# Starting the second group's front end inside the first group's serial chain, and reordering the first transfers

## The chip, the cores and the metric

The kernel runs on one core of one Trainium2 chip. The metric is the device time of one execution in microseconds (us); lower is better. TensorE is written PE below, VectorE DVE, ScalarE ACT, GpSimd POOL, and SyncE, which issues most of the DMAs, SP.

## The reference, cut to what matters

The input is 16 sequences of 256 tokens with 128 channels, 4096 tokens in all, in float32. A Mamba layer is followed by a small dense FFN, and then by eight experts that every token goes through:

```python
xz = layernorm(x) @ in_proj_w.T;  xi, z = split(xz)             # 256 + 256 channels
xc = silu(causal_conv4(xi) + conv_b)                            # per channel, 4 taps
dt, B, C = split(xc @ x_proj_w.T, [8, 24])                      # 8 + 16 + 16 columns
dt = softplus(dt @ dt_proj_w.T + dt_proj_b)
h_t = exp(dt_t * A) * h_(t-1) + dt_t * B_t * xc_t               # 16 states per channel
y_t = sum_n h_t[n] * C_t[n]
x1 = x + ((y + D * xc) * silu(z)) @ out_proj_w.T
x2 = layernorm(x + x1 + relu(layernorm(x1) @ w1.T + b1) @ w2.T + b2)
out = layernorm(x2 + sum over 8 experts of (silu(x2 @ Wg[e]) * (x2 @ Wu[e])) @ Wd[e])
```

## The kernel before, in words

The tokens are cut into eight **groups** g of 512 tokens (two sequences). Channels or states lie on the 128 partitions and tokens on the free axis, so nearly every tile is 128x512 floats. For each group there are four pieces of work, written as Python generators that issue some instructions and `yield`:

- `stage_a(g)`: layer norm (statistics on DVE at L167 to L171, a power on POOL at L173, `nb` on DVE at L179, the normalised `xh` on ACT at L185), four transposes on PE into `pxn`, `xn` on ACT (L244). Then two `stage_conv` generators, one for each half of the 256 inner channels: a projection `pi` on PE (L316), the first tap `hc` on ACT (L319), three more taps on DVE (L326), a tanh on ACT (L334), and `xc` on DVE (L336). Then `pd` on PE (L262), its copy `dbc` on ACT (L267), a store of the 32 rows of B and C to a DRAM tile `bc`, issued by ACT (L270), two `pv` matmuls (L276), `dt` on ACT (L278), its softplus on ACT with a table load (L282), `u` on POOL (L286), and the gate `zg` from `pz` (L298, L304, L307).
- the **scan**: 32 states k for each group, 16 for each half. `fetch` (L347) loads B and C from `bc`, broadcast to all partitions, for two states at a time, 512 KB each, into three buffers. `front` makes `dA` on ACT (L354) and `dBx` on POOL (L356, four buffers). `back` runs the recurrence on DVE (L362) and multiplies with C (L364, `hC`). `sum_states` transposes each `hC` into the sum `y` on PE (L369).
- `stage_c(g)`: gate, output projection `po`, norm, FFN (`pf`, `pff`), norm, and the transposed result `x2T` (L478).
- the **experts**: 32 slices j for each group; each makes `pg` and `pu` on PE (L488, L490), tanh and copy on ACT, two products on DVE and POOL, and adds to `acc` on PE (L518).

The order on each engine is written out by hand: the schedule is manual and engines run their instructions in program order. A prologue runs `stage_a(0)` alone until its `dt` and `u` are there (`while "ready" not in ...`, L549). Then comes one main loop (L567); each pass issues one scan state, and one expert slice when a group's `x2T` exists, and advances the generators in `running` by fixed half steps. `limit[0]` caps how many PSUM banks the generators may hold, through `take`. Group g+1 is prepared while group g is scanned; `stage_a(1)` starts in pass k = 1 of group 0, `stage_a(g+1)` in pass 11 of group g for the others. Expert slices of group 0 run beside the scan of group 1, and so on.

All loads of inputs stand at the head of SP's queue: x of groups 0 and 1, the small weights, and then the eight experts with three transfers of 256 KB each (L143 to L146). The first `fetch` calls (L555) come after those 24 in SP's order:

```python
for k in range(0, FETCH, NC):
    fetch(0, k)
```

Of the kernel before, what the change touches and what calls it, by code (L numbers as in the profile page):

```python
# [9 lines left out]
AF = mybir.ActivationFunctionType  # L10
# [8 lines left out]
KC = 4  # L19
# [3 lines left out]
NE = 8  # L23
NF = 4
NC = 2
# [5 lines left out]
FETCH = 4  # L31
START_A = 11
NB = 4
EPS = 1e-5
FAR = 1e28
SLOW = 1e-25
# [3 lines left out]
def kernel(  # L40
# [99 lines left out]
    wg = const.tile([P, NE, NF * P], FP, tag="wg", name="wg")  # L140
    wu = const.tile([P, NE, NF * P], FP, tag="wu", name="wu")
    wd = const.tile([P, NE, NF, DM], FP, tag="wd", name="wd")
    for e in range(NE):  # L143
        nc.sync.dma_start(out=wg[:, e, :], in_=Wg[e])
        nc.sync.dma_start(out=wu[:, e, :], in_=Wu[e])
        nc.sync.dma_start(out=wd[:, e], in_=Wd[e].rearrange("(f p) d -> p f d", p=P))  # L146

    def prepare():

# [57 lines left out]
    def done(name):  # L207
        held.remove(name)
        give(name)
# [15 lines left out]
    def stage_a(g):  # L225
        xt = x_tiles[g]
        s = state[g] = {}
        yield
        stats = norm_stats(xt, f"a{g}")
        yield  # L230
        yield
        scale = norm_shift(stats, f"a{g}")
        yield
        xh = wide("xh", f"xh{g}", 2)
        norm_apply(xt, as4(xh), scale)
        yield
        if g > 0:
            yield
            yield
        pt = yield from take(f"pxn{g}")  # L240
        transpose(pt, as4(xh))
        yield
        xn = wide("xn", f"xn{g}", 2)
        nc.scalar.activation(xn, pt, AF.Identity, bias=b1_sb[:, 0:1], scale=g1_sb[:, 0:1])  # L244
        done(f"pxn{g}")
        yield
        s["xc"] = act.tile([P, NH, TB], FP, tag="xc", name=f"xc{g}")
        for h in range(NH):
            conv = stage_conv(g, h, xn)
            next(conv)  # L250
            next(conv)
            running.append([conv, False])
        while (NH - 1) not in s.get("conv", ()) or 0 not in s["conv"]:
            yield
            yield
        if g > 0:
            yield
            yield
        R = DTR + 2 * NS
        pd = yield from take(f"pd{g}")  # L260
        for h in range(NH):
            nc.tensor.matmul(  # L262
                pd[0:R, :], lhsT=xpw[:, h, :], rhs=s["xc"][:, h, :], start=(h == 0), stop=(h == NH - 1)
            )
        yield
        dbc = act.tile([R, TB], FP, tag="dbc", bufs=1, name=f"dbc{g}")
        nc.scalar.copy(dbc, pd[0:R, :])  # L267
        done(f"pd{g}")
        bc = s["bc"] = dram.tile([2 * NS, TB], FP, tag="bc", name=f"bc{g}")
        nc.scalar.dma_start(out=bc, in_=dbc[DTR:R, :])  # L270
        yield
        dt = s["dt"] = act.tile([P, NH, TB], FP, tag="dt", name=f"dt{g}")
        u = s["u"] = act.tile([P, NH, TB], FP, tag="u", name=f"u{g}")
        for h in range(NH):
            pv = yield from take(f"pv{g}_{h}")
            nc.tensor.matmul(pv, lhsT=dtw[:, bass.ts(h, P)], rhs=dbc[0:DTR, :], start=True, stop=True)  # L276
            yield
            nc.scalar.activation(dt[:, h, :], pv, AF.Identity, bias=dtb[:, h : h + 1])  # L278
            done(f"pv{g}_{h}")
            if h == 0:  # L280
                yield
        nc.scalar.activation(dt, dt, AF.Softplus)  # L282
        yield
        zg = s["zg"] = act.tile([P, NH, TB], FP, tag="zg", name=f"zg{g}")
        for h in range(NH):
            nc.gpsimd.tensor_tensor(u[:, h, :], dt[:, h, :], s["xc"][:, h, :], ALU.mult)  # L286
            if h == NH - 1:

                nc.gpsimd.memset(dt.rearrange("p h (b l) -> p (h b) l", l=L)[:, :, 0:1], FAR)
                s["ready"] = True  # L290
            elif g > 0:
                yield
                yield
        for h in range(NH):

            pz = yield from take(f"pz{g}_{h}")
            for c in range(NTT):
                nc.tensor.matmul(  # L298
                    pz[:, bass.ts(c, P)], lhsT=xn[:, bass.ts(c, P)], rhs=inw[:, bass.ts(NH + h, P)],
                    start=True, stop=True,  # L300
                )
            yield
            tz = wide("tz", f"tz{g}_{h}", 1)
            nc.scalar.activation(tz, pz, AF.Tanh, scale=0.5)  # L304
            yield

            nc.vector.scalar_tensor_tensor(zg[:, h, :], tz, 1.0, pz, ALU.add, ALU.mult)  # L307
            done(f"pz{g}_{h}")
        yield

    def stage_conv(g, h, xn):

        s = state[g]
        yield
        pi = yield from take(f"pi{g}_{h}")
        nc.tensor.matmul(pi, lhsT=inw[:, bass.ts(h, P)], rhs=xn, start=True, stop=True)  # L316
        yield
        hc = wide("hc", f"hc{g}_{h}", 2)
        nc.scalar.activation(  # L319
            hc, pi, AF.Identity, bias=cb[:, h : h + 1], scale=cw[:, h, KC - 1 : KC]  # L320
        )
        yield
        hv = hc.rearrange("p (b l) -> p b l", b=NSEQ)
        pv = pi.rearrange("p (b l) -> p b l", b=NSEQ)
        for k in range(1, KC):
            nc.vector.scalar_tensor_tensor(  # L326
                hv[:, :, k:], pv[:, :, : L - k], cw[:, h, KC - 1 - k : KC - k], hv[:, :, k:],
                ALU.mult, ALU.add,
            )
            if g > 0 and k == KC - 2:  # L330
                yield
                yield
        yield
        nc.scalar.activation(pi, hc, AF.Tanh)  # L334
        yield
        nc.vector.scalar_tensor_tensor(s["xc"][:, h, :], pi, 1.0, hc, ALU.add, ALU.mult)  # L336
        done(f"pi{g}_{h}")
        s.setdefault("conv", set()).add(h)
        yield
# [209 lines left out]
    while "ready" not in state.get(0, {}):  # L549
        if rounds == 1:  # L550
            running.append([prepare(), False])
        half()
        half()
        rounds += 1
    for k in range(0, FETCH, NC):  # L555
        fetch(0, k)
    skip(0, 0)
    for k in range(AHEAD):
        front(0, k)
# [7 lines left out]
    while added < NG * NJ or running:  # L567
        in_scan = t < len(scans)
        in_experts = j < len(slices)
        limit[0] = 1 if in_experts else 2  # L570
        if in_scan:
            g, k = scans[t]
            if k == 0 and 0 < g and g + 1 < NG:
                load_x(g + 1)
            if k == (START_A if g > 0 else 1) and g + 1 < NG:
                running.append([stage_a(g + 1), False])
            t2 = t + FETCH
            if t2 < len(scans) and t2 % NC == 0:
                if "bc" not in state.get(scans[t2][0], {}):
                    raise ValueError("B and C are fetched before they are made")  # L580
                fetch(*scans[t2])
        half()
        if in_experts:
            up(*slices[j])
        half(quick=True)
        half(quick=True)
        lag = LAG_Y if in_experts else 1
        while summed <= min(t - lag, len(scans) - 1):
            gs, ks = scans[summed]
            if ks % NS == 0 and summed:  # L590
                gb, kb = scans[summed - 1]
                gate(gb, kb // NS)
                launch(stage_y(gb, 0) if kb // NS == 0 else stage_c(gb), kb // NS == 1)
            sum_states(gs, ks)
            summed += 1
            if summed == len(scans):
                gate(gs, 1)
                launch(stage_c(gs), True)
        if j > multiplied:
            hidden(*slices[multiplied])  # L600
            multiplied += 1
        if in_scan:
            back(g, k)
            t2 = t + AHEAD
            if t2 < len(scans):
                front(*scans[t2])
                if t2 + 1 < len(scans) and scans[t2 + 1][1] % NS == 0:
                    skip(scans[t2 + 1][0], scans[t2 + 1][1] // NS)
        if in_experts:
            half_gate(*slices[j])  # L610
            j += 1
        if added < (multiplied - 1 if in_experts else multiplied):
            gd, jd = slices[added]
            down(gd, jd)
            added += 1
            if jd == NJ - 1:
                launch(stage_e(gd))
        half()
        if not in_experts:
            half(quick=True)  # L620
            half(quick=True)
        if queued < NG and "x2T" in state.get(queued, {}):
            slices += [(queued, n) for n in range(NJ)]
            queued += 1
        t += 1
# [44 lines left out]
```

## Time and profile before

| | |
|---|---|
| median of three runs | 1095.85 us (1095.71 to 1100.99) |
| the profiled execution | 1096.13 us, its span 1094.3 us |
| busy share of the span | PE 90%, DVE 72%, POOL 65%, ACT 59% |
| mean granted PE clock | 0.952 |
| DMA | 147.03 MB, mean 134 GB/s |
| first instruction of the recurrence (L362) | 35.76 us after the span's start |
| last `hC` of group 0 (L364) | starts at 109.67 us |
| `x2T` of group 0 (L478) | starts at 144.06 us |

A timeline row has the start, the duration, the engine, the source line, the operation, what it writes and reads, the shapes and a count; in brackets stands how long the engine was idle before it and what released it. "SPq" and "ACTq" are DMA issues: they show when a transfer was issued, not when it landed. A windows row has a stretch of the span, its length, the busy time (and instructions) of PE, PEld, DVE, ACT and POOL in this order, the granted PE clock, the DMA engines' busy share, and GB/s. In the page the strips of digits are tenths for 40 equal slices of the span, 27.4 us each.

### The profile page before, as it was taken

How to read it: one execution, taken by the hardware profiler on the slowest of the kernel's cores; microseconds unless marked ns; L12 is line 12 of the kernel's file. 1: busy time of each engine (PE TensorE's matmuls, PEld its weight loads, DVE VectorE, ACT ScalarE, POOL GpSimd, SP SyncE). 2: the span in 40 equal slices, each digit the busy share in tenths (PEclk: the TensorE clock that was granted, in tenths of full speed). 3: DMA queues.
4: the chain of work that ended last, by engine and by line, in shares of the span. 5: the costliest groups of instructions: out<-in, count | busy, mean ns of one | idle time of the engine just before them, and what ended most of it. 6: DMA issues, size and time to landing. Idle time of an engine off the chain costs nothing.

```text
span 1094.3 us, 11408 instructions
## 1 busy us (share of the span) xinstructions
PE 989.5 (90%) x3488; PEld 516.7 (47%) x3488; DVE 786.0 (72%) x1211; ACT 642.0 (59%) x1091; POOL 710.3 (65%) x591
## 2 busy tenths in 40 slices
PE   4356689997999989999999999999999999999996
PEld 2234545454445554455445554455445555544442
DVE  2689489686897779686987789686987678724222
ACT  3453357754667656755767656655667656544543
POOL 0656367675777757676778667676778668644543
PEclk9575789998999999999999999999999999999998
DMA  8857444352444334452444434452454434100000
GB/s 239 300 192 250 147 154 153 130 190 78 164 157 159 132 117 150 136 185 84 157 163 158 133 118 144 144 176 92 152 169 140 144 124 164 58 0 1 10 1 10
DMA packets 56269, 147.03 MB, mean 134 GB/s; under 512 B 7688, under 2 KB 20880, under 8 KB 56208
## 3 DMA queue, kind: packets, MB, share of 16 engines
q1 hardware_dynamic: 51600, 143.69, 39.5%
q10 hardware_dynamic: 4608, 2.62, 0.8%
q8 instruction: 27, 0.44, 0.2%
q14 instruction: 34, 0.28, 0.1%
HBM read 143.67 MB, written 2.62 MB: 134 GB/s over the span
## 4 chain that ended last, share of the span: by engine, by line
PE 46%; DVE 11%; ACT 3%; issue 2%; POOL 1%; ACTq 0%; POOLq 0%
PE pg L488 11%; PE pu L490 11%; PE acc L518 11%; PE y L369 5%; DVE dA L362 3%; PE pff L455 2%; DVE v L503 2%; PE pf L447 2%; DVE hC L364 1%; ACT x L185 1%; PE po L414 1%; PE pv L276 1%; DVE hc L326 1%; ACT x1h L185 1%; PE pd L262 1%
## 5 line engine op out<-in xcount | busy, mean ns | idle before, releaser
L510 POOL TENSOR_TENSOR v<-v,us 128x512 f32<-128x512 f32 x256 | 324.8, 1270 | 156.4 <-ACT us L494 95.5
L356 POOL TENSOR_TENSOR dBx<-B,u 128x512 f32<-128x512 f32 x256 | 325.1, 1272 | 22.9 <-DVE dA L362 12.1
L362 DVE TENSOR_TENSOR_SCAN dA<-dA,dBx 128x512 f32<-128x512 f32 x256 | 313.1, 1223 | 19.9 <-POOL dBx L356 16.8
L503 DVE SCALAR_TENSOR_TENSOR v<-eth,pg 128x512 f32<-128x512 f32 x256 | 174.9, 683 | 184.6 <-ACT eth L492 184.5
L488 PE MATMUL pg<-x2T,wg 128*128 128x512 f32 x512 | 265.8, 601 | 0.0
L490 PE MATMUL pu<-x2T,wu 128*128 128x512 f32 x512 | 263.8, 597 | 1.9 <-ACT us L494 1.9
L518 PE MATMUL acc<-v,wd 128*128 128x512 f32 x512 | 262.1, 594 | 1.5 <-POOL v L510 1.5
L492 ACT ACTIVATE eth<-pg 128x512 f32<-128x512 f32 x256 | 152.2, 595 | 163.5 <-PE pg L488 159.8
L354 ACT ACTIVATE dA<-dt,A 128x512 f32<-128x512 f32 x256 | 177.6, 694 | 103.5 <-DVE hC L364 101.7
L369 PEld LDWEIGHTS y<-ident,hC 128*128 128x128 f32 x1024 | 133.7, 150 | 149.4 <-issue 100.6
L369 PE MATMUL y<-ident,hC 128*128 128x128 f32 x1024 | 168.1, 291 | 36.1 <-DVE hC L364 36.1
L364 DVE TENSOR_TENSOR hC<-dA,C 128x512 f32<-128x512 f32 x256 | 177.1, 692 | 10.8
L494 ACT COPY us<-pu 128x512 f32<-128x512 f32 x256 | 149.8, 585 | 55.7 <-PE pu L490 55.3
L490 PEld LDWEIGHTS pu<-x2T,wu 128*128 128x128 f32 x512 | 97.0, 191 | 127.7 <-issue 108.3
L488 PEld LDWEIGHTS pg<-x2T,wg 128*128 128x128 f32 x512 | 92.5, 193 | 101.0 <-issue 72.8
L518 PEld LDWEIGHTS acc<-v,wd 128*128 128x128 f32 x512 | 80.3, 191 | 22.1 <-issue 17.6
L173 POOL TENSOR_TENSOR rs_c<-ve_c,mhalf 128x4 f32<-128x4 f32 x8 | 8.1, 1017 | 70.4 <-DVE ve_c L171 70.4
L286 POOL TENSOR_TENSOR u<-dt,xc 128x512 f32<-128x512 f32 x16 | 20.3, 1269 | 41.5 <-ACT dt L282 41.5
L326 DVE SCALAR_TENSOR_TENSOR hc<-pi,cw,hc 128x510 f32<-128x510 f32 (+2 forms) x48 | 35.4, 743 | 6.3 <-ACT hc L319 5.6
L462 DVE TENSOR_TENSOR res<-pff,res 128x512 f32<-128x512 f32 x8 | 5.5, 692 | 42.5 <-PE pff L455 42.5
L173 POOL TENSOR_TENSOR rs_b<-ve_b,mhalf 128x4 f32<-128x4 f32 x8 | 8.1, 1007 | 42.1 <-DVE ve_b L171 42.1
L447 PE MATMUL pf<-h,w 128*128 128x512 f32 x64 | 34.5, 627 | 0.9 <-ACT h L441 0.9
(84 smaller groups left out, 655.9 us busy)
## 6 DMA issues: line engine op xcount, KB each, us to landing
B<-bc SPq DMA_DIRECT2D x128, 512.0 KB, 4.8
C<-bc SPq DMA_DIRECT2D x128, 512.0 KB, 3.9
xt<-in_x_dram SPq DMA_DIRECT2D x8, 256.0 KB, 4.5
wg<-in_Wg_dram SPq DMA_DIRECT2D x8, 256.0 KB, 6.0
wu<-in_Wu_dram SPq DMA_DIRECT2D x8, 256.0 KB, 5.9
wd<-in_Wd_dram SPq DMA_DIRECT2D x8, 256.0 KB, 6.1
out_dram<-x ACTq DMA_DIRECT2D x8, 256.0 KB, 4.8
bc<-dbc ACTq DMA_DIRECT2D x8, 64.0 KB, 2.8
```

The lines of the kernel that those rows point to most:

```text
L354: nc.scalar.activation(dA, s["dt"][:, h, :], AF.Exp, scale=A_sb[:, h, n : n + 1])
L356: nc.gpsimd.tensor_tensor(dBx, s["B", k // NC][:, k % NC, :], s["u"][:, h, :], ALU.mult)
L362: nc.vector.tensor_tensor_scan(dA, dA, dBx, 0.0, ALU.mult, ALU.add)
L364: nc.vector.tensor_mul(hC, dA, s["C", k // NC][:, k % NC, :])
L369: nc.tensor.matmul(y[:, bass.ts(c, P)], lhsT=src[:, bass.ts(c, P)], rhs=ident, is_transpose=True, start=first and c == 0, stop=last and c ...
L488: nc.tensor.matmul(pg, lhsT=wg[:, e, bass.ts(f, P)], rhs=s["x2T"], start=True, stop=True)
L490: nc.tensor.matmul(pu, lhsT=wu[:, e, bass.ts(f, P)], rhs=s["x2T"], start=True, stop=True)
L492: nc.scalar.activation(th, pg, AF.Tanh, scale=0.5)
L494: nc.scalar.copy(us, pu)
L503: nc.vector.scalar_tensor_tensor(v, th, 1.0, pg, ALU.add, ALU.mult)
L510: nc.gpsimd.tensor_tensor(v, v, us, ALU.mult)
L518: nc.tensor.matmul(s["acc"], lhsT=wd[:, e, f, :], rhs=s.pop(("h", j)), start=(j == 0), stop=(j == NJ - 1))
```

## The change

Three things are altered. `stage_a(1)` is started in round 4 of the prologue rather than in pass 1 of the main loop, and for the first two groups the extra waiting steps (`if g > 0: yield; yield`) are dropped, both `pv` matmuls are issued before the two `dt` activations, and generators may hold three banks outside the experts. `fetch(0, 0)` and `fetch(0, 2)` are issued as soon as the store to `bc` exists. Experts 6 and 7 are loaded in the first two passes of group 1's scan, after the load of x for group 2.

```diff
+NEARLY = 6
...
-    for e in range(NE):
+    def load_expert(e):
         nc.sync.dma_start(out=wg[:, e, :], in_=Wg[e])
         nc.sync.dma_start(out=wu[:, e, :], in_=Wu[e])
         nc.sync.dma_start(out=wd[:, e], in_=Wd[e].rearrange("(f p) d -> p f d", p=P))
+    for e in range(NEARLY):
+        load_expert(e)
...
-        if g > 0:      # three places in stage_a and one in stage_conv
+        if g > 1:
             yield
             yield
...
+        pvs = []
         for h in range(NH):
             pv = yield from take(f"pv{g}_{h}")
             nc.tensor.matmul(pv, lhsT=dtw[:, bass.ts(h, P)], rhs=dbc[0:DTR, :], start=True, stop=True)
-            yield
-            nc.scalar.activation(dt[:, h, :], pv, AF.Identity, bias=dtb[:, h : h + 1])
-            done(f"pv{g}_{h}")
+            pvs.append(pv)
+            if h == 0 and g < 2:
+                continue
+            yield
+            for i, pv in enumerate(pvs, h + 1 - len(pvs)):
+                nc.scalar.activation(dt[:, i, :], pv, AF.Identity, bias=dtb[:, i : i + 1])
+                done(f"pv{g}_{i}")
+            pvs = []
...
     while "ready" not in state.get(0, {}):
         if rounds == 1:
             running.append([prepare(), False])
+        if rounds == 4:
+            running.append([stage_a(1), False])
         half()
         half()
+        if "bc" in state[0] and ("B", 0) not in state[0]:
+            for k in range(0, FETCH, NC):
+                fetch(0, k)
         rounds += 1
-    for k in range(0, FETCH, NC):
-        fetch(0, k)
...
-        limit[0] = 1 if in_experts else 2
+        limit[0] = 1 if in_experts else NB - 1
...
-            if k == (START_A if g > 0 else 1) and g + 1 < NG:
+            if t in range(NK, NK + NE - NEARLY):
+                load_expert(NEARLY + t - NK)
+            if k == START_A and 0 < g and g + 1 < NG:
                 running.append([stage_a(g + 1), False])
```

In the resulting program the orders of all engines differ only in the prologue and in group 0's first states; from state 16 of group 0 on, PE, DVE, ACT and POOL run the same instructions in the same order as before. On DVE the order around the first recurrence becomes: the three taps of both halves of group 0, the norm statistics of group 1, the two `xc` of group 0, `nb` of group 1, all six taps of group 1, then recurrence 0, `hC` 0, `zg` of half 0, the two `xc` of group 1, recurrence 1, and so on. On ACT: `xh` of group 1 stands before the copy `dbc` of group 0; `xn` of group 1 before `dt` of group 0; the two `hc` of group 1 between the softplus of group 0 and its `dA` 0; and the two `dt` of group 1, its softplus and the table loads on either side of it now stand between `dA` 4 and `dA` 5 of group 0 (before: between `dA` 14 and `dA` 15).

More of the change, by code (lines that the diff above doesn't have):

```diff
@@ L255, in stage_a @@
             yield
-        if g > 0:
+        if g > 1:
             yield
@@ L290, in stage_a @@
                 s["ready"] = True
-            elif g > 0:
+            elif g > 1:
                 yield
@@ L329, in stage_conv @@
             )
-            if g > 0 and k == KC - 2:
+            if g > 1 and k == KC - 2:
                 yield
```

## The prediction

> **What bounds the kernel now.** I read the page first:
>
> ```profile
> span 1094.3 us, 11408 instructions
> PE   4356689997999989999999999999999999999996
> DVE  2689489686897779686987789686987678724222
> PEclk9575789998999999999999999999999999999998
> ```
>
> From slice 6 or 7 on (about 145 us, where `x2T` of group 0 is made) PE is at nine tenths nearly everywhere: the experts bind there. In slices 2 to 5 PE has 3 to 6 tenths, DVE up to 9, and the granted PE clock is low. This front part is a serial lead-in; what shortens it moves all the rest forward, since every engine's order after it is unchanged. The timeline of the front part, in rows far apart:
>
> ```profile
> 21.84 0.58 ACT L267 COPY dbc<-pd 40x512 f32<-40x512 f32 x1 [3.63 <-PE pd L262]
> 23.38 0.36 ACTq L270 DMA_DIRECT2D bc<-dbc  x1
> 28.76 0.33 SPq L347 DMA_DIRECT2D B<-bc  x1
> 34.47 5.04 POOL L356 TENSOR_TENSOR dBx<-B,u 128x512 f32<-128x512 f32 x4 [4.20 <-DMA B<-bc]
> 35.76 1.23 DVE L362 TENSOR_TENSOR_SCAN dA<-dA,dBx 128x512 f32<-128x512 f32 x1 [16.83 <-POOL dBx L356]
> 40.69 0.86 DVE L167 BATCH_NORM_STATS2 st_a<-xt 128x6 f32<-128x128 f32 x4
> 51.94 2.96 DVE L326 SCALAR_TENSOR_TENSOR hc<-pi,cw,hc 128x510 f32<-128x510 f32 x4
> 56.75 1.39 DVE L326 SCALAR_TENSOR_TENSOR hc<-pi,cw,hc 128x506 f32<-128x506 f32 x2
> 71.51 1.28 ACT L282 ACT_TABLE_LOAD   x1
> 75.97 1.23 DVE L362 TENSOR_TENSOR_SCAN dA<-dA,dBx 128x512 f32<-128x512 f32 x1 [2.89 <-ACT dA L354]
> 109.67 0.69 DVE L364 TENSOR_TENSOR hC<-dA,C 128x512 f32<-128x512 f32 x1
> 123.34 1.26 POOL L356 TENSOR_TENSOR dBx<-B,u 128x512 f32<-128x512 f32 x1
> 144.06 0.59 ACT L478 COPY x2T<-px 128x512 f32<-128x512 f32 x1 [0.57 <-PE px L192]
> ```
>
> DVE idles 16.83 us before the first recurrence: that waits for `dBx`, which waits for B. From 35.76 to 110.28 (the instruction after the last `hC`) DVE is nearly full; a state costs 1.925 us (12 states from 87.16 to 110.28). Between the states stand group 1's norm and taps, and one 2.89 us stall while ACT does group 1's softplus with its tables. The windows view shows two more things:
>
> ```profile
> 34.00:36.00 2.00, 0.00 (x0) 0.00 (x0) 0.24 (x1) 0.00 (x0) 1.53 (x2) 0.50 1.01 410
> 262.00:268.00 6.00, 3.79 (x24) 2.60 (x22) 2.27 (x11) 0.00 (x0) 1.31 (x2) 1.00 0.07 26
> 268.00:278.00 10.00, 5.88 (x16) 3.93 (x17) 8.96 (x18) 4.63 (x9) 4.41 (x4) 0.50 0.29 105
> ```
>
> The DMA engines are full while B lands, and between the experts of groups 0 and 1 PE idles (6.33 us, then half clock): there group 1's own chain is late. It hangs on the same lead-in, so it moves along.
>
> [...]one pass of a 128x512 matmul took 0.85 us at 18 us and 0.43 us at 50 us. [...]the 64 KB store to `bc` took 4.9 us among the weights, 2.8 us in the median. [...]the trace has 1.28 us and the next activation 0.01 us behind, so I use 1.29.
>
> **The change, part by part.** Times are those of the profiled execution.
>
> *Store, B and C.* The norm of group 1 goes in front of group 0's `xc` on DVE: four statistics, four aggregates and one add, 1.26 us (40.69 to 41.95). `xc` is finished at 20.0 instead of 18.93, `pd` 1.1 later, `dbc` at 23.5 instead of 22.42. The store was held until 23.38 by its semaphore's earlier transfer, so it moves only to 23.6. With 4.9 us it lands at 28.5. SP passes six transfers fewer (its last weight issue is at 22.6 instead of 27.8), so the `bc` landing alone decides: B goes out near 28.9, as before. What changes is what lies ahead of it: 1.57 MB of weights, 4.3 us at the 360 GB/s of that stretch, are gone. B lands after its shortest time in this trace, 3.7 us, at 32.6 instead of 34.4. The early `fetch` call alone changes little.
>
> *dt and u.* Four transposes (`pxn` of group 1, about 1 us) stand between `pd` and `pv`: `pv` starts near 24.1 instead of 22.47, the softplus ends at 29.2 instead of 27.54, `u` (two of 1.27) at 31.8 instead of 30.1. The group's `xh` (1.63 us on ACT) fills ACT's 3.63 us wait for `pd`: free. Then ACT has two `hc` (1.6) and `skip` (0.7) before the exp table (1.29): `dA` 0 is ready at 33.6 instead of 31.0.
>
> *First recurrence.* Six taps now stand ahead of it on DVE: they start behind the first `hc` at 30.05 and take 6 x 0.742 (12.98 to 17.43) = 4.45: 34.5. `dBx` would be ready at 33.9, `dA` at 33.6. So 34.5 instead of 35.76: **-1.2**. With PE at full clock through `pv` it is 33.9, with half clock throughout 35.8.
>
> *DVE work that leaves the states*: norm 1.26, `nb` 0.49, four taps 2.88 (51.94 to 54.82), two taps 1.30: **-5.9**. It now lies in the 16.83 us of idling, which ended with B. Group 1's `xc` and `zg` stay between the states.
>
> *The table stall moves to state 5.* DVE's work from recurrence 0 to 5 is 5 x 1.925 + 2.9 (three `zg`, two `xc`) = 12.5: due at 47.0. ACT: `pd` of group 1 starts at 38.3, once DVE has `xc`, and takes 1.7 (full clock) to 3.4; `dbc` 0.6; two `pv` 1.7 to 3.4; the second `dt` 0.7; table, softplus, table 3.65; `dA` 5 0.7; `tz` 0.6, for whose `zg` DVE waits ahead of recurrence 5; `zg` 0.6. With gaps of 0.6 that is 49.2 to 52.6. PE was mostly idle just before, so half clock at first: I take 51.0, a stall of 4.0 instead of 2.9, and 0.1 less elsewhere: **+1.0**. Behind the waiting `zg` stands all of DVE; POOL's `u` (2.5 us from the end of the softplus, 47.8, on) delays `dBx` 6 to 51.7, while recurrence 6 is due at 53.5: hidden.
>
> *Experts 6 and 7.* Six issues of 0.45 us on SP ahead of B and C of states 4 and 6 of group 1, and 4.3 us of transfer. That B was issued at 107.43 and landed within 6.4 (113.9 at the latest); now some 2.5 later. Its `dBx` runs at 123.34, behind the norm of stage C on POOL: 7 us are left. B of state 6, about 4 later, is used near 126: about 5 left. Zero; should they be late after all, up to 4.3. Expert 6 is used 24 slices after `x2T`. Three banks instead of two: no instruction moves by it.
>
> Sum: -1.2 - 5.9 + 1.0 = -6.1; the last `hC` of group 0 ends near 104.2 instead of 110.3. Stage C (34 us to `x2T`) and all later work keep their order and move with it. The profiled execution took 1096.13 us, 0.28 over the median of 1095.85; against the median I forecast 1095.85 - 6.1 = **1089.8 us**. Bounds: full clock in both stretches gives 33.9 + 12.5 and a stall of 2.2 (49.2 less 47.0), so recurrence 5 at 48.6 and -8.5; half clock in both gives 35.8 + 12.5 + 5.6 = 53.9 and -3.2. [...]2 us either way, an estimate from 0.5 us for each us at half clock.
>
> **The rivals.**
>
> *Late clock, late `dt` (18%).* PE stays at half clock for `pv` of group 0 and for `pd` and `pv` of group 1. For it: the granted clock is 0.50 from 26 us on, and PE still idles between pieces. Against it: PE now has `pd`, `pxn`, `pv` and `pi` almost without a gap. Time: 1095.85 - 3.2 = 1092.6.
>
> *The front part is not what counts (5%).* If group 1's chain at 262 to 272 us had another limit, the gain would vanish: 1095.8. Against it: between 145 and 262 us PE, DVE and ACT keep their order and PE has no idling to give back.
>
> *Slower: half-clock stretches in the PE-bound part (8%).* [...]price: 5.1 us for each 10.24 us (0.5 each); it decides from 12 us of additional half clock, where -6.1 is used up. One of the three runs, 1100.99, is 5.1 over the others, just one such stretch. Three more give 1095.85 - 6.1 + 15.4 = 1105.1. [...]against: the two other runs agree within 0.14 us.
>
> *More than forecast (7%).* `bc` lands sooner with fewer weights behind it, and PE has its full clock in both stretches: 1095.85 - 8.5 = 1087.3.
>
> **How the numbers follow.** Half a per cent, 5.5 us, is about what a measurement of this kernel can tell from no change. The forecast's case has 62%; its own range is -4.5 to -7.5, and 53 of the 62 are beyond 5.5. With the 7% that is 0.60 faster. Within: 9 + 18 + 5 + 2 of the slower case = 0.34. Slower: 0.06. The range goes from 1086.0 (-8.5 with 1.3 us of luck in stage C) to 1094.5 (-3.2 with 1.9 us of bad luck): it leaves out the slower case, most of the one without gain, and the ends.
>
> **What would show it.** Right: the first recurrence at 34 to 35 us, no norm or taps of group 1 between states, one stall of 3 to 5 us before recurrence 5, the last `hC` of group 0 at 103 to 106, `x2T` some 6 us earlier, PE as full as before after it. Wrong: a first recurrence after 36, a second stall between states 5 and 31, `dBx` of group 1 waiting for B behind the experts, or a longer half-clock stretch than at 268 to 278 us.

## The result, and the profile after

The changed kernel takes 1087.17 us (median of four runs, 1086.55 to 1088.77); the kernel before took 1097.15 beside it. The ratio is 0.9904, 95% interval 0.9887 to 0.9921: faster by about 10 us, where 6.1 were forecast. The profiled execution took 1086.55 us, 9.58 less than the one of before; it is the lowest of the four.

The page's strips after (40 slices of 27.1 us):

```profile
span 1084.8 us, 11409 instructions
PE   4656699997999989999999999999999999999996
DVE  3798589686978599686978599686987688724222
PEclk9755899998999999999999999999999999999999
```

From slice 6 on PE is as full as before. The timeline of the front part, in rows far apart:

```profile
23.67 0.36 ACTq L275 DMA_DIRECT2D bc<-dbc  x1
28.44 0.33 SPq L358 DMA_DIRECT2D B<-bc  x1
29.45 4.53 DVE L337 SCALAR_TENSOR_TENSOR hc<-pi,cw,hc 128x510 f32<-128x510 f32 x6 [9.32 <-ACT hc L330]
32.79 2.49 POOL L367 TENSOR_TENSOR dBx<-B,u 128x512 f32<-128x512 f32 x2 [1.29 <-DMA B<-bc]
34.10 1.23 DVE L373 TENSOR_TENSOR_SCAN dA<-dA,dBx 128x512 f32<-128x512 f32 x1
44.10 1.28 ACT L293 ACT_TABLE_LOAD   x1
49.00 0.69 DVE L318 SCALAR_TENSOR_TENSOR zg<-tz,pz 128x512 f32<-128x512 f32 x1 [3.04 <-ACT tz L315]
49.61 1.23 DVE L373 TENSOR_TENSOR_SCAN dA<-dA,dBx 128x512 f32<-128x512 f32 x1
101.84 0.69 DVE L375 TENSOR_TENSOR hC<-dA,C 128x512 f32<-128x512 f32 x1
134.98 0.59 ACT L489 COPY x2T<-px 128x512 f32<-128x512 f32 x1 [0.57 <-PE px L197]
```

Line numbers are 11 higher than before in this region. The first recurrence has no bracket: six taps (29.45 to 33.98) and `dBx` 0 (to 34.06) end within 0.1 us of each other just ahead of it, where before DVE idled 16.83 us, at the end for B; 9.32 us of that idling are left, ahead of the taps. No norm or tap of group 1 stands between the states any more; one stall is left, 3.04 us ahead of recurrence 5, which waits for ACT's `tz` behind the softplus and its two table loads. The last `hC` of group 0 starts at 101.84 instead of 109.67, and `x2T` at 134.98 instead of 144.06.

Two more figures sort all that follows. **Stage C** is taken from the start of the last `hC` of group 0 to the start of its `x2T`: 34.39 us before, 33.14 after. **The rest** runs from that `x2T` to the end of the execution: 952.07 before, 951.57 after. So of the 9.58 us, 7.83 come before stage C, 1.25 in it and 0.50 later.

### The profile page after: what moved, and what is told of

Read it like the earlier page. It is cut to its first block, busy times and chain, and to the rows that moved or that the text cites. A ratio compares the mean times of both kernels' runs of the same rounds, so it can differ in the third digit from the quotient of the medians.

```text
span 1084.8 us, 11409 instructions
## 1 busy us (share of the span) xinstructions
PE 989.3 (91%) x3488; PEld 517.2 (48%) x3488; DVE 785.6 (72%) x1211; ACT 641.5 (59%) x1091; POOL 710.2 (65%) x591
## 4 chain that ended last, share of the span: by engine, by line
PE 44%; DVE 13%; ACT 3%; issue 2%; POOL 1%; ACTq 0%; POOLq 0%
PE pg L499 11%; PE pu L501 11%; PE acc L529 11%; PE y L380 4%; DVE dA L373 3%; DVE v L514 2%; PE pff L466 2%; PE pf L458 2%; DVE hC L375 2%; ACT x L190 1%; PE po L425 1%; PE pv L282 1%; DVE hc L337 1%; ACT x1h L190 1%; PE pd L267 1%
```

## Experiments

My theory was that the gain is DVE work laid into an idle stretch (the larger part) and B landing sooner (the smaller). The rivals: the transfers are the gain; or the part after the states gains by itself. Runs that were made together share a chip and the runs of the kernel before; other sets ran on other chips, so between sets I compare ratios to the kernel before, or traces, not microseconds.

### The halves of the change, each by itself

```diff
 # front_only: the changed kernel
-NEARLY = 6
+NEARLY = 8
 # transfers_only: the kernel before, with load_expert(), NEARLY = 6, the two
 # late loads and the early fetch; stage_a(1) still starts in pass 1
```

> The changed kernel with all eight experts loaded at the head again (NEARLY = 8): only the early start of the second group's front end is left of the change. Theory (the larger part of the gain is DVE work that lies in an idle stretch, the smaller part is B landing sooner): B waits behind 1.57 MB of weights again and lands near 34.4 us as before, dBx 0 ends near 35.7, the first recurrence stands at 35.7 instead of 34.1, the last hC of group 0 at 103.4, and the whole at 1087.2 + 1.6 = 1088.8 us, 8.3 below the kernel before. Rival (the transfers are the gain): near the kernel before, over 1094. Rival (the transfers do nothing, the six taps alone set the first recurrence): first recurrence at 34.1 and 1087.2 us.

> The kernel before with only the other half of the change: experts 6 and 7 loaded in the first two passes of group 1's scan, and B and C fetched right behind their store; the second group's front end stays where it was. Theory: without the norm and the taps of group 1 ahead of it the first recurrence waits for B alone, which lands near 32.5 instead of 34.4; dBx 0 at 33.8, so 33.8 to 34.0 instead of 35.76, all else in place, and the whole 1.9 us below the kernel before, 1095.2 us. Rival (the transfers are the gain): 8 us or more below it. Rival (experts 6 and 7 delay B of group 1): no gain or a loss, with dBx of group 1 waiting for B.

Measured: front_only 1090.24 us, ratio 0.9931 (0.9918 to 0.9944); transfers_only 1095.41 us, ratio 0.9979 (0.9971 to 0.9986), both beside 1097.95. The two ratios multiply to 0.9910, and the whole change has 0.9904: the halves add up, and the front end is about three quarters of it. The rival "the transfers are the gain" is out. (front_only keeps the early `fetch` calls, the order of `pv` and `dt` and the third bank; none of these was run by itself.)

In transfers_only the recurrence waits for B through `dBx` alone, and comes where it was expected (DVE's timeline):

```profile
33.70 1.23 DVE L366 TENSOR_TENSOR_SCAN dA<-dA,dBx 128x512 f32<-128x512 f32 x1 [14.61 <-POOL dBx L360]
```

In front_only the first recurrence was late by more than expected, 36.15 instead of 35.7, and two things came late together (timeline, ACT, PE, DVE and POOL rows):

```profile
24.14 3.78 PE L282 MATMUL pv<-dbc,dtw 8*128 8x512 f32 x4
25.11 0.78 ACT L249 ACTIVATE xn<-pxn,b,g 128x512 f32<-128x512 f32 x1 [1.33 <-DMA wd<-in_Wd_dram]
27.95 0.69 ACT L288 ACTIVATE dt<-pv,dtb 128x512 f32<-128x512 f32 x1 [1.02 <-PE pv L282]
31.71 4.53 DVE L337 SCALAR_TENSOR_TENSOR hc<-pi,cw,hc 128x510 f32<-128x510 f32 x6 [11.54 <-ACT hc L330]
34.78 2.50 POOL L367 TENSOR_TENSOR dBx<-B,u 128x512 f32<-128x512 f32 x2 [1.02 <-DMA B<-bc]
36.15 1.22 DVE L373 TENSOR_TENSOR_SCAN dA<-dA,dBx 128x512 f32<-128x512 f32 x1
```

The first is `pv` at half clock: it took 3.78 us where the changed kernel's took 1.98, and started 0.46 later. The second `dt` waited for it, and the softplus, `hc` and the taps all came 2.26 us later. The second is B, about as late: `dBx` 0 ended at 36.05 instead of 34.06. ACT's issue of the store stood at 24.70 instead of 23.67; by the trace it was held for a weight transfer, and `xn`, behind it in ACT's queue, with it. That delayed B, issued at 29.75 instead of 28.44, but not the taps: ACT still had to wait for `pv` afterwards. An execution of softplus_later_busy (an experiment further down, with six early experts) has the slow `pv` without a held store, and its taps started as late, at 31.95:

```profile
24.05 0.36 ACTq L281 DMA_DIRECT2D bc<-dbc  x1
24.38 3.78 PE L288 MATMUL pv<-dbc,dtw 8*128 8x512 f32 x4
```

So in this pair the later weights bring B sooner, in part by freeing the store's issue. The slow `pv` is not shown to be their doing: transfers_only, with six early experts, has it too.

### Four experts late

```diff
-NEARLY = 6
+NEARLY = 4
```

> The changed kernel with four experts loaded late instead of two (NEARLY = 4). Theory: B lands another 4 us sooner, but the six taps of group 1 end at 34.0 as before, so dBx 0 is ready 1 to 1.5 us before its recurrence and the first recurrence stays at 34.0 to 34.1; the last hC of group 0 and the whole do not move, 1087.2 us within 0.5. Rival (B still ends the wait): first recurrence at 33 or earlier and 1086. Rival (late loads collide with B and C of group 1): dBx of states 32 and later waits for B by some us, and the whole is 1 to 4 us longer.

Measured: 1088.10 us, ratio 0.9905 (0.9891 to 0.9919), against 0.9904 of the changed kernel: no change. POOL's timeline shows that B has left the path:

```profile
31.73 6.30 POOL L367 TENSOR_TENSOR dBx<-B,u 128x512 f32<-128x512 f32 x5
```

Here `dBx` starts without a wait, right behind `u` and a small memset, 1.06 us sooner than after; B was issued at 25.66 instead of 28.44. The recurrence stays at 34.18, behind the taps. POOL waited 3.7 us for B between 92 and 126 us instead of 0.8, but not because of the late loads: these B were issued by 95.39, ahead of the first late load at 99.68, and the kernel before waits 4.4 us in that stretch. Behind the late loads no `dBx` waited for B there: they are hidden, as forecast.

### The softplus a pass later

```diff
+        if g == 1:          # ahead of the softplus, and again ahead of the gates
+            yield
+            yield
         nc.scalar.activation(dt, dt, AF.Softplus)
```

> The changed kernel with two more half steps ahead of group 1's softplus and two more ahead of its gates: on ACT dA 5 now precedes the two table loads, and zg of group 1 stands behind hC 6 and hC 7 on DVE. Theory (the 3.04 us stall ahead of recurrence 5 is ACT's chain table load, softplus, table load, dA, tanh, and DVE has too little work queued to cover it): ACT starts the table load near 44.8 and has dA 6 at 49.1, DVE has finished hC 5 at 47.8, so one stall of 1.3 us is left, ahead of recurrence 6; the last hC of group 0 comes 1.7 us sooner, at 100.1, and the whole is 1085.5 us. Rival (the stall is given back in stage C[...]): the last hC 1.7 us sooner but the whole anywhere between 1084 and 1088. Rival (dBx or u is what is late there): recurrence 6 or 7 waits for dBx, and nothing is gained.

Measured: 1088.80 us, ratio 0.9916 (0.9902 to 0.9930). The stall shrank to 1.54 us (1.3 expected), the last `hC` came 1.0 us sooner than after (its lead-in was 0.5 later in this execution), and the whole was no shorter (DVE's and ACT's timeline). From the first recurrence to the last `hC` it took 66.22 us instead of 67.74:

```profile
49.95 1.23 DVE L379 TENSOR_TENSOR_SCAN dA<-dA,dBx 128x512 f32<-128x512 f32 x1 [1.54 <-ACT dA L371]
135.93 0.59 ACT L495 COPY x2T<-px 128x512 f32<-128x512 f32 x1 [0.57 <-PE px L197]
```

From the last `hC` at 100.84 to this `x2T` are 35.09 us, not 33.14: stage C took the gain back, with 17.1 us of half clock between 113 and 141 us where after has 13.7 between 114 and 139. And the rest was 952.98 us, 1.4 longer. One place of that is seen in the windows view (the third figure from the end is the granted clock). First after, then this kernel, at the same work behind `pao` of group 1:

```profile
396.00:398.00 2.00, 1.76 (x7) 1.07 (x8) 1.97 (x3) 1.56 (x5) 2.00 (x3) 1.00 0.00 0
```

```profile
396.00:398.00 2.00, 1.82 (x6) 1.19 (x7) 1.97 (x3) 1.55 (x5) 2.00 (x3) 0.66 0.01 2
398.00:400.00 2.00, 2.00 (x3) 0.56 (x2) 1.07 (x3) 0.82 (x2) 0.97 (x1) 0.50 0.26 78
```

The same idling of 2.96 us ahead of `pao` was followed by full clock in one and by a stretch of half clock in the other. A second such stretch began at 963.2 us. The half-clock stretches of stage C don't begin with the work: in after they run for 6.8 us from 114.9, 0.8 us ahead of `ph`, and for 6.8 us from 132.0, 1.3 us ahead of `px`; PE idled when each began. From here on the question was how much of any time in this study is made by such stretches.

### Keeping PE busy where it idles

The filler is a transpose of the identity into a PSUM bank that nothing reads at that time; it feeds nothing.

```diff
+    def busy(n, into=None):
+        for i in range(n):
+            nc.tensor.transpose((spare if into is None else into)[:, bass.ts(i % NTT, P)], ident, ident)
 # busy_stage_c: busy(8) in passes 30 to 32, busy(24) behind po and behind pff of group 0
 # busy_boundary: busy(36, pt) ahead of pao of group 0
 # softplus_later_busy: busy_stage_c with the later softplus
 # all_together: all of these, NEARLY = 4, and busy(22) behind both pi of group 0
```

> The changed kernel plus transposes of the identity into a PSUM bank that nothing reads then (the later acc), which keep PE busy around stage C of group 0: 8 in each of three passes ahead of it, 24 behind po and 24 behind pff. Theory (stage C of group 0 is a serial chain whose PE steps run at half clock wherever PE idled just before[...]): ph and px take 0.65 instead of 1.63, pf 0 1.0 instead of 2.07, pyt and the first y 0.6 instead of 1.06; x2T comes 29 to 30 us behind the last hC instead of 33.1, and the whole is 3.5 us shorter, 1083.6. Rival (PE's steps are not what the chain waits for, DVE, ACT and POOL are): 33 us and 1087. Rival (the filler stands in the way of the chain's own steps): longer than 33.1.

> The changed kernel plus 36 transposes of the identity into pao's own bank ahead of pao of group 0, in the 6.3 us in which PE waits between the experts of group 0 and those of group 1. Theory (the half-clock stretch behind that gap costs half its length): the stretch at half clock near 262 to 268 us is gone and the whole is 3.4 us shorter, 1083.8. Rival (the chain of group 1 on DVE and ACT limits the first slices there anyway): clock full but the whole at 1086 to 1087.

> The later softplus of softplus_later and the filler of busy_stage_c together. Theory (softplus_later did bring the last hC 1 us sooner[...]): with PE kept busy stage C is as long as in busy_stage_c, and the sooner hC now shows: 1.0 to 1.7 us below busy_stage_c, about 1082. Rival (the later softplus or gates delay something else): no shorter than busy_stage_c.

> The changed kernel with everything that should help: four experts late, the later softplus, the fillers of busy_stage_c and busy_boundary, and 22 more transposes behind both pi of group 0, which cover the 5.6 us in which PE waits for xc. Theory: pd of group 0 takes 1.8 instead of 3.5 us, so the six taps and the first recurrence come 1.7 us sooner, near 32.4; the last hC of group 0 near 98.4, x2T near 128, no half clock at the boundary; the whole near 1076.5 us. Rival (POOL's u or B then ends the wait): first recurrence at 33 or later and 1077 to 1079. Rival (the fillers in the prologue run into pd): first recurrence at 34 or later.

Measured, beside 1098.43: busy_stage_c 1086.71, ratio 0.9892 (0.9878 to 0.9907); busy_boundary 1089.38, 0.9915 (0.9901 to 0.9929); softplus_later_busy 1085.12, 0.9887 (0.9869 to 0.9904); all_together 1083.23, 0.9855 (0.9836 to 0.9874). Only the last is apart from the changed kernel's 0.9904, and it missed its 1076.5 by far. Its profiled execution is the slowest of its four, 1087.16 us. The traces show two reasons.

*Too little filler.* A transpose takes 0.11 us at full clock (36 took 4.09 us in busy_boundary), not the 0.15 I had read from groups of four, so 24 ended 2.1 to 2.2 us ahead of `ph` and of `px`; the clock fell, and stage C took 32.9 us in busy_stage_c. The 22 ahead of `pd` in all_together left 2.12 us, and `pd` took 3.52, as after. The 36 ahead of `pao` left 2.42 us in two kernels; the clock held in busy_boundary and fell in all_together, where `pao` took 1.12 instead of 0.66 (PE's timeline of busy_stage_c, busy_boundary and all_together, a row each):

```profile
115.36 1.63 PE L197 MATMUL ph<-ident,x1h 128*128 128x128 f32 x4 [2.12 <-ACT x1h L190]
262.55 0.66 PE L197 MATMUL pao<-ident,ao 128*128 128x128 f32 x4 [2.42 <-ACT ao L542]
262.33 1.12 PE L197 MATMUL pao<-ident,ao 128*128 128x128 f32 x4 [2.42 <-ACT ao L554]
```

*The gain given back elsewhere.* In busy_boundary the boundary did run at full clock (PE's timeline: `pg` there took 1.12 us instead of 2.08), and `x2T` of group 2 came 1.9 us sooner after that of group 0. Then half-clock stretches came at 394.6 to 398.0 and at 961.3 to 964.7 us, which the changed kernel's execution did not have:

```profile
264.32 1.12 PE L505 MATMUL pg<-x2T,wg 128*128 128x512 f32 x2 [0.24 <-ACT x2T L495]
394.61 1.88 PE L505 MATMUL pg<-x2T,wg 128*128 128x512 f32 x2
```

From the times of `x2T` the two cost 0.7 us (group 2 to 3: 122.87 instead of 122.18) and 1.7 (group 6 to 7: 107.95 instead of 106.25). The last interval has only these two values, within 0.01 us, in all ten executions profiled so far, and it has the longer one in just the four that show this stretch: busy_boundary, softplus_later, busy_stage_c, all_together.

softplus_later_busy was 1.6 us below busy_stage_c, as its theory had it, but the two ratios overlap, and its profiled execution does not show the theory: the last `hC` came later there, at 102.46, behind the slow `pv` and a first recurrence at 36.40, and stage C was 32.21 instead of 32.94 us. That test is left to the next set.

### Filler in every such place

```diff
 # busy_all: the changed kernel, and
+        busy(8)          in passes 29 to 32
+        busy(40, pt)     ahead of ph and of px of group 0; 12 ahead of ph of group 7
+        busy(7, pf)      ahead of pf 0 of group 0
+        busy(54, pt)     ahead of pao of group 0; 20 ahead of pao of group 1
 # busy_all_softplus: and the later softplus
 # busy_all_front: and NEARLY = 4, and busy(34) behind both pi of group 0
```

> The changed kernel plus filler transposes of the identity in every place where PE was seen to idle ahead of a half-clock stretch: 8 in each of four passes ahead of stage C of group 0, 40 ahead of its ph and of its px (24 left 2.1 to 2.2 us of idling and the clock fell), 7 ahead of its first pf, 54 ahead of pao of group 0, 20 ahead of pao of group 1 (busy_boundary fell to half clock there at 394.5 to 398.5 us), 12 ahead of ph of the last group (half clock at 961 to 965 us in four of the runs). Theory (beyond the first group's states the time is the same PE-bound program, longer by half of each 3.4 us window at half clock[...]): no half clock between stage C of group 0 and the last group's end, stage C 31 instead of 33.1 us, the boundary 1.9 us shorter and nothing given back at 395 or 962; 1082.5 us, and the runs of this kernel nearer to each other than the 2 to 4 us of the runs so far. Rival (full clock there is given back to the other engines, whose work ends no sooner): 1086 to 1087.

> The fillers of busy_all and the later softplus of softplus_later. Theory: the last hC comes 1.0 to 1.7 us sooner than in busy_all and, with the clock held, this reaches the end: 1081 us. Rival (the later softplus costs elsewhere): the same as busy_all or longer.

> busy_all_softplus with four experts late and 34 filler transposes behind both pi of group 0 (22 left 2.1 us of idling ahead of pd, which then took 3.5 us as before). Theory: pd of group 0 at full clock, 1.8 us instead of 3.5; dbc, the store, dt, the taps and the first recurrence 1.7 us sooner, at 32.4; the whole 1079.3 us. Rival (the fillers run at half clock and end after 19.5, ahead of pd): first recurrence at 34 or later and 1081 us or more. Rival (pi of group 1 then falls to half clock): half of the gain.

Measured, beside 1097.95: busy_all 1080.81, ratio 0.9851 (0.9834 to 0.9868); busy_all_softplus 1079.46, 0.9841 (0.9824 to 0.9858); busy_all_front 1077.69, **0.9821 (0.9805 to 0.9838)**, the best of the study. From stage C of group 0 on no half clock is left but in the last group's tail, after 1071 us. Stage C and the rest are now the same to within 0.1 us in all three (times in us):

| kernel (profiled execution) | last `hC` | stage C | the rest |
|---|---|---|---|
| before | 109.67 | 34.39 | 952.07 |
| transfers_only | 107.78 | 34.33 | 952.13 |
| after | 101.84 | 33.14 | 951.57 |
| front_only | 103.88 | 33.15 | 951.61 |
| four_late | 101.96 | 33.40 | 951.80 |
| softplus_later | 100.84 | 35.09 | 952.98 |
| busy_stage_c | 101.98 | 32.94 | 952.55 |
| busy_boundary | 101.65 | 33.15 | 952.45 |
| softplus_later_busy | 102.46 | 32.21 | 951.46 |
| all_together | 100.15 | 33.80 | 953.21 |
| busy_all | 102.00 | 30.65 | 948.02 |
| busy_all_softplus | 100.64 | 30.64 | 948.01 |
| busy_all_front | 99.28 | 30.65 | 948.08 |

PE's and ACT's timeline of busy_all, at the filler, the first `pf` (2.07 us in after) and the end of stage C:

```profile
110.47 4.53 PE L203 MATMUL ph<-ident 128*128 128x128 f32 x40
117.73 1.12 PE L468 MATMUL pf<-h,w 128*128 128x512 f32 x2
132.65 0.58 ACT L501 COPY x2T<-px 128x512 f32<-128x512 f32 x1 [0.42 <-PE px L197]
```

With the clock held behind the states, the later softplus brings 1.36 us at the last `hC` and 1.35 in the median, though the runs of the two kernels overlap by half a microsecond. From the first recurrence to the last `hC` it takes the same 1.5 us away with filler (67.74 to 66.22) as without: the gain was there in softplus_later too. busy_all_front, with the filler in front of `pd` and four experts late, brings another 1.36 at the last `hC` and 1.77 in the median, through the taps, which now start at 28.40; four experts late alone had moved nothing (PE's and DVE's timeline of busy_all_front):

```profile
19.78 1.91 PE L275 MATMUL pd<-xc,xpw 128*40 128x512 f32 x4 [0.65 <-DVE xc L361]
32.84 1.22 DVE L387 TENSOR_TENSOR_SCAN dA<-dA,dBx 128x512 f32<-128x512 f32 x1
```

The four runs of busy_all_front lie within 1.45 us of each other; the nine of the kernel before, in the same set, within 4.06.

### The kernel before with the same filler

> The kernel before with the fillers of busy_all at the same places, and nothing of the change. Theory (the change itself is worth 7.7 to 7.8 us, the shift of the last hC of group 0, and the 2 us more that the runs show came from half-clock windows that fell otherwise): stage C 30.65 us and 948.0 us from x2T of group 0 to the end, as in the three kernels with fillers; last hC at 109.7, so 109.7 + 30.65 + 948.0 = 1088.4 us, 7.6 above busy_all. Rival (the change also shortens stage C and later work by itself): 2 us more, 1090.4 us or above, with stage C longer than 30.65 or the rest longer than 948.

This is the kernel before with the fillers of busy_all and nothing of the change. Measured: 1089.86 us (1088.35 to 1091.70), ratio 0.9911 (0.9894 to 0.9927). Stage C took 30.65 us and the rest 948.22: both as in the changed kernels with filler, so the rival is out: with the clock held, the change does nothing behind the last `hC` of group 0. Only the lowest of the six runs is at the expected 1088.4; in the profiled one, the highest, the last `hC` came at 112.83, not 109.7 (PE, POOL and DVE rows of its timeline):

```profile
22.69 3.77 PE L282 MATMUL pv<-dbc,dtw 8*128 8x512 f32 x4 [0.67 <-ACT dbc L273]
36.11 5.13 POOL L362 TENSOR_TENSOR dBx<-B,u 128x512 f32<-128x512 f32 x4 [3.81 <-DMA B<-bc]
112.83 0.69 DVE L370 TENSOR_TENSOR hC<-dA,C 128x512 f32<-128x512 f32 x1
```

`dBx`, waiting for B, started 1.64 us later than in the first execution of before; 0.55 us of waiting stood ahead of group 1's taps, and the waits between states 13 and 15 grew from 3.06 to 3.93 us, with more of `pd` and `pz` of group 1 at half clock. The lead-in of the kernel before varies by itself.

## Why the prediction was right, and where its sizes were off

The direction, the part that gains and the order of the waits were right. The size was not: the forecast was 6.1 us of 1095.85, 0.56%, and the measured ratio says 0.96%. That is more than the forecast's own range of 4.5 to 7.5 us, and more than the 8.5 of its bound at full clock; the last `hC`, foreseen at 103 to 106, came at 101.84 and ended at 102.53. Against the two profiled executions:

| term | forecast | measured |
|---|---|---|
| first recurrence | -1.2 | -1.66 (35.76 to 34.10) |
| DVE work between the states | -5.9 | -5.91 (busy 68.83 to 62.92 us from the first recurrence to the end of the last `hC`) |
| DVE's waits in that stretch | +1.0 | -0.26 (the stall 3.04 instead of 2.89; a second of 0.17 gone; gaps of 0.1 us and less for the rest) |
| last `hC` of group 0 | -6.1 | -7.83 |
| stage C and later | 0, within 2 | -1.75 |
| the whole | -6.1 | -9.58 |

**The moved DVE work** was right to 0.01 us: the instructions and durations of the rows, added up, and a cover (16.83 us of idling) that was long enough.

**The first recurrence** was a near tie as forecast, and 0.4 sooner, but a tie of two: the taps began at 29.45 instead of 30.05, since the two `dt` and the softplus ended 0.4 earlier, and `dBx` 0 ended last, at 34.06, with the taps at 33.98. `dA` 0 had started at 32.01, ready well ahead of both. `pv` at full clock was foreseen as possible and not as certain; where it ran at half clock (front_only, softplus_later_busy) the recurrence came at 36.15 and 36.40.

**The stall** is the term that was mis-sized most: +1.0 against -0.02 for the two waits named. I took the middle between half and full clock for `pd` and `pv` of group 1. `pd` started at 37.40, nearly a microsecond before my 38.3, and PE went to full clock at 39.83, within it; `pv` took 1.98 us for both (PE's timeline of after):

```profile
37.40 3.09 PE L267 MATMUL pd<-xc,xpw 128*40 128x512 f32 x4 [0.42 <-DVE xc L347]
41.16 1.98 PE L282 MATMUL pv<-dbc,dtw 8*128 8x512 f32 x4
```

That put the table load at 44.10 and recurrence 5 at 49.61 instead of 51.0. My bound for full clock, 48.6, was nearer. The mechanism, what waits for what, was as described.

**Stage C and later.** "0, within 2 us" covers the -1.75; the 2 us were an estimate for half-clock stretches that fall otherwise, at 0.5 us for each us at half clock. The fillers turn this from an argument into a measurement: with PE held at full clock, stage C and the rest are alike in the kernel before and in the changed ones (30.65, and 948.0 to 948.2 us). So the 1.75 us are not less work; they come from where the half-clock stretches fall. Whether that is chance is open, and the profiles speak against pure chance: without filler up to that `x2T` and without the later softplus, the four kernels with the early front end have a stage C of 33.14 to 33.40 us (after, front_only, busy_boundary, four_late), the two others 34.39 and 34.33. In three of the four the first half-clock stretch of stage C began 13.1 us behind the last `hC`, although the half-clock stretches begin at other times in each execution; before and transfers_only have 15.0 and 14.9. The stretches can also take: softplus_later lost 3.4 us there against after.

**What the change is worth with PE's clock held from stage C on** stays known only within limits. The last `hC` says 7.8 us between the first two profiles and 10.8 between before_busy_all and busy_all, since the lead-in of the kernel before varies too; the ratios of these two to the kernel before, 0.9911 and 0.9851, give 0.994, about 6.6 us with some 2.6 either way.

**The rivals.** "Late clock" did not come to pass in the changed kernel's profile, but it is real: front_only, transfers_only, softplus_later_busy and before_busy_all have `pv` at 3.8 us. "Slower by half-clock stretches" is real too, and its price was right in kind (in busy_boundary a stretch of 3.4 us cost 1.7 us at 961 and 0.7 at 394); but these two were of 3.4 us each, not of 10, and PE had idled only 1.60 and 2.96 us ahead of them. "Experts 6 and 7: zero" held, and held with four. "More than forecast" gave 1087.3, where the median lies, but by its own reasons only in part: the stall and the first recurrence were better than the middle that I took, by 1.5 us together, and most of the rest comes from stage C and later, where the forecast had put nothing. The held store of the kernel before (23.38) was in the forecast; that with eight early experts it is held again at the later time, as in front_only, was not.

## What to carry to other kernels

Work that is moved into an idle stretch can count in full, if each queue that it is moved past is walked through; here DVE's busy time gave it to 0.01 us. A gain of one to two microseconds ahead of a chain with a half-clock matrix engine can't be read from the total: measure at the last instruction of the changed stretch, or hold the clock with filler in every idle place first, and then compare. Filler should reach close to the next real step: with 0.3 to 0.8 us left the clock held in every place here; with 2.1 to 2.4 us left it fell in most places and held in one (`pao` of busy_boundary). And before a delay is put down to a held queue, look at what the next instruction in that queue waited for.

## What was not expected of the hardware

- PE fell to half clock after 2.1 us of idling (24 fillers ahead of `ph`), after 2.42 us (`pao` of group 0, in all_together and not in busy_boundary) and after 2.96 us (`pao` of group 1, in some executions and not in others), and the idling of 1.60 us ahead of the last group's `ph`, with four transposes spread over the next 1.5 us, was followed by it too (busy_boundary, from 961.3).
- One stretch of half clock in PE-bound work at 961 us costs 1.70 us, half of its 3.4, and from group 3 to group 6 the intervals between two `x2T` are otherwise the same within 0.06 us in all kernels.
- ACT's store issue waited, by the releaser that the trace names, for a weight transfer of SP's queue (1.33 us of idling on ACT, front_only), with all of ACT behind it.
- Transposes of 128x128 floats in a row take 0.11 us each at full clock (36 in 4.09 us, busy_boundary) and 0.21 at half (8 began 1.71 us ahead of the step behind them, busy_stage_c at 99.78); four of them between other work read as 0.60.
